# Rows of every expert slot turned by DMA under the shared expert, and loaded three slots ahead

## The chip, the core and the metric

The kernel runs on one core of a Trainium2 chip. The time is the device time of one execution in microseconds (us). Several runs of a kernel differ by a few us (three runs of this one: 2012.39 to 2018.24), so the median counts. A profile is one execution with the hardware profiler. TensorE (PE in the profile) multiplies matrices, and its weight loads are listed apart (PEld); VectorE is DVE, ScalarE ACT, GpSimd POOL, and SyncE (SP) issues most plain DMAs. Results of TensorE lie in PSUM banks and must be read out by VectorE or ScalarE.

## What is computed

Four sequences of 1024 tokens, 1024 wide, pass a cross-attention and a mixture of experts. Cut to what matters here:

```python
x = x + xattn(layernorm(x), ctx, Wq, bq, Wk, bk)      # softmax over 1024 context rows
xt = layernorm(x).reshape(4096, 1024)
scores = sigmoid(xt @ gate_w.T)                        # 8 experts
_, sel = top_k(scores + expert_bias, 2)
sel_flat = sel.reshape(-1)
order = argsort(sel_flat, stable=True)                 # 8192 rows, sorted by expert
tok_idx = order // 2
routed_in = xt[tok_idx] * top_scores.reshape(-1)[order][:, None]
routed_out = grouped_swiglu(routed_in, w1, w2, w3, rows_per_expert)   # bf16, hidden 704
shared = silu(xt @ sw1.T) * (xt @ sw3.T) @ sw2.T       # float32
x = x + shared.at[tok_idx].add(routed_out)
```

## The kernel before

There are three stages, and TensorE works through them almost without a gap.

**Attention** (to about 640 us). 32 groups of 128 tokens are handled in 16 steps p of two groups. Beside the products (`product`, L401, with the seven block products of `seven`, L199) each step normalizes, routes, and scatters the weighted tokens as bf16 rows into the DRAM table `xrows`, in a region for each expert (`scatter`, L525; each row carries its token's number behind the 1024 values). `convert(e)` (L244) lets GpSimd issue three DMAs that copy expert e's float32 weights to bf16 tables in DRAM; L650 calls it in steps 1, 5, 9 and 13, for experts 0 to 3.

**Shared expert** (640 to 1473 us). 8 blocks s of 512 tokens (NJ = 8, loop at L1100), in float32. `up(s)` (L937) makes the hidden activations: one product for the tails (`pt_c`, 7.06 us) and five rounds f of the seven products with halves (12.09 us a round, 1.73 us a product). `down_pair(s, 0)` and `down_pair(s, 1)` (L1033) make the outputs, two sets of seven products, some 18 us each. `between(k)` is called after product k and puts the work of VectorE and ScalarE there. `block(s + 1)` (L154) loads the next block's tokens (`xb`) on SyncE's queue once `up(s)` has read the old ones, GpSimd forms sums of them (`differences`, L174), and `residuals(s)` (L996) loads 2 MB of `x2c` at round 1. Experts 4 to 7 are converted at L1134 in blocks 0 to 3, between the two down pairs.

Under this stage the rows of the expert stage are prepared by the generator `turns` (L1001). The routed rows are taken in 23 **slots** (NS) of 512 rows, each with one expert, each of four **turns** of 128 rows. A turn: GpSimd gathers 128 rows from `xrows` into `xgt` (four buffers, asked for two turns ahead; L750 is the line of every gather), VectorE takes the token numbers out of it (`toks`, L1022), and SyncE issues a DMA transpose of the 128 x 1024 values into half of `xh` (L1027). After two turns `xh` is stored to DRAM (L1019): the store stands in SyncE's queue ahead of the next turn's transpose, and waits for both transposes of its pair. L974 takes one turn after products 1 and 4 of each round, from block 2 on: 10 turns in each of six blocks, 60, the rows of slots 0 to 14 (NTURN = 15).

**Experts** (1473 us to the end; loop at L1176). Each slot is an up part (88 matmuls at L131, from the turned rows `xTb` and the gathered weights `w`) and a down part (L1161, L1167, L1169). A slot's row count sets the width of its matmuls at run time, so slots take 13 to 29 us. Two sets of buffers (`bps`) alternate. After its up part a slot issues: for slots below 15, on SyncE, the load of slot s+2's turned rows as two DMAs (`fetch_turned`, L906, L909), into the buffer that was just read; and on GpSimd the gather of slot s+2's w13 (`fetch_up`). GpSimd then adds the 512 output rows into `out` by indirect DMAs (L1208) and gathers w2 and w2t of slot s+2 (`fetch_down`). Gathers whose expert the buffer already holds move nothing. Slots 15 to 22 are not turned by DMA: `fetch_rows` (L882) gathers their rows into SBUF, and during the up part of the slot before, `turned_rows` (L911) lets TensorE transpose eight 128 x 128 pieces per turn through PSUM (L920), which VectorE copies out (L921).

TensorE, GpSimd, and in these stages VectorE, ScalarE and SyncE keep the order in which the program is written: an instruction that waits holds up all that are behind it on its engine or queue.

Of the kernel before, what the change touches and what calls it, by code (L numbers as in the profile page):

```python
# [29 lines left out]
BF16 = mybir.dt.bfloat16  # L34
# [26 lines left out]
EPS = 1e-5  # L61
LEAST = 32
ROW = D + 32
NTURN = 15


_WIDTHS = dict(ident=P, tri=P, ones=P, before=E * E, upto=E * E, region=E, expert=E, full=NJ,
# [12 lines left out]
def xattn_moe_kernel(ctx: ExitStack, tc: tile.TileContext, x, ctxT, wqT, wkT, bqk, gwT, ebias,  # L80
# [14 lines left out]
    def const(k):  # L95
        return con[:, _AT[k][0] : _AT[k][1]]

    ident = const("ident")
    identb, trib, onesb = (cp.tile([P, P], BF16, name=f"{k}b") for k in ("ident", "tri", "ones"))
    before = const("before").rearrange("p (i j) -> p i j", j=E)  # L100


# [14 lines left out]
    ps_t = ctx.enter_context(tc.tile_pool(name="ps_t", bufs=2, space=PSUM))  # L117
# [111 lines left out]
    with ExitStack() as a:  # L229
# [316 lines left out]
        load(0)  # L546
        with tc.manual_schedule(engines=vector_scalar):
            ps_e = psum("ps_e", 3)
            for dst, k in ((identb, "ident"), (trib, "tri"), (onesb, "ones")):
                nc.vector.tensor_copy(dst, const(k))  # L550
            halves = queries(0)
            tokens(0)
# [32 lines left out]
            for p in range(NT // 2):  # L585
# [35 lines left out]
                def between(k):  # L621
# [15 lines left out]
                    elif k == 1:  # L637
                        if new:
                            looked(i)
                            softened(i)  # L640
                        if not ahead:
                            gss[g - 2] = gate_parts(g - 2, xtTs.pop(g - 2))
                        elif p:
                            xtTs[g - 1] = turn(g - 1)
                        if ahead:
                            scaled(b + 1, i, on_scalar=True)
                        if p > 1:
                            tois, ss = listing.pop(g - 4)
                            listing[g - 4] = tois, [weighted(g - 4, j, ss) for j in range(G)]
                        if p % (NT // E) == 1:  # L650
                            convert(p // (NT // E))
                    elif k == 2:
                        if not ahead:
                            xtTs[g - 1] = turn(g - 1)
                        looked(i + 1)
                        softened(i + 1)
                        if g + 2 < NT:
                            norms[g + 2] = statistics(xin[g + 2], f"1_{g + 2}")
                        if g + 2 == NT:
                            two_sums.close()  # L660
                            cps.append(pool(shared, "c3"))
                            block(0)
                    elif k == 3:
                        if p:
                            gss[g - 1] = gate_parts(g - 1, xtTs.pop(g - 1))
                            lg = ps_s.tile([P, G, E], F32, tag="lg", name=f"lg_{g}")
                            gate(lg, g - 2, gss.pop(g - 2))
                        if ahead:
                            turned(b + 1, i)
                            scaled(b + 1, i + 1, on_scalar=True)  # L670
                        if p:
                            gate(lg, g - 1, gss.pop(g - 1))
                            routing[g - 2] = route(g - 2, lg)
                        if p > 1:
                            scatter(g - 4, *listing.pop(g - 4))
                        if g + 2 < NT:
                            norms[g + 3] = statistics(xin[g + 3], f"1_{g + 3}")
                    elif k == 4:
                        if ahead:
                            turned(b + 1, i + 1)  # L680
                    elif k == 5:
                        if g + 2 < NT:
                            tokens(g + 2)
                        if p:
# [71 lines left out]
    def tables(tb):  # L756
# [123 lines left out]
    weights, fetched, slots = [], {}, {}  # L880
# [22 lines left out]
    def xT_of(s):  # L903
        return bps[s % 2].tile([P, KC, SLOT], BF16, tag="xT", name=f"xTb_{s}")

    def fetch_turned(s):  # L906
        slots[s] = xT_of(s), tokens_of[s]
        for h in range(2):
            nc.sync.dma_start(slots[s][0][:, :, h * 2 * P : (h + 1) * 2 * P], xturned[s][h])  # L909

    def turned_rows(s, q):  # L911
        if q == 0:
            slots[s] = xT_of(s), bps[s % 2].tile([P, NQ], I32, tag="toks", name=f"toks_{s}", bufs=2)
        xT, toks = slots[s]
        xg = fetched[s][q]
        nc.vector.tensor_tensor(toks[:, q : q + 1], xg[:, D : D + 2].bitcast(I32),
                                beyond[:, s, q : q + 1], ALU.bitwise_or)
        pt = ps_t.tile([P, KC, P], BF16, tag="pt", name=f"ptb_{s}_{q}")
        for c in range(KC):
            nc.tensor.transpose(pt[:, c, :], xg[:, c * P : (c + 1) * P], identb)  # L920
        nc.vector.tensor_copy(xT[:, :, q * P : (q + 1) * P], pt)  # L921

    def widths(s):

# [7 lines left out]
    with shared, tc.manual_schedule(engines=vector_scalar | {mybir.EngineType.SP}):  # L932
# [4 lines left out]
        def up(s):  # L937
# [3 lines left out]
            for f in range(NF):  # L941
# [11 lines left out]
                def between(k):  # L953
# [46 lines left out]

        def turns():  # L1001

            blocks = list(itertools.product(range(NTURN), range(NQ)))
            asked = []

            def ask(s, q):
# [8 lines left out]
            for j, (s, q) in enumerate(blocks):  # L1015
# [10 lines left out]
                    xh = tr.tile([P, KC, 2 * P], BF16, tag="xh", name=f"xh_{s}_{h}", bufs=2)  # L1026
                nc.sync.dma_start_transpose(xh[:, :, v * P : (v + 1) * P], xg[:, :D])  # L1027
                if v:
                    done = xturned[s][h], xh
                yield  # L1030
            nc.sync.dma_start(*done)

        def down_pair(s, u, more=None):  # L1033
# [23 lines left out]
            def between(k):  # L1057
# [21 lines left out]
                if more:  # L1079
                    more(k)  # L1080

# [18 lines left out]
        for s in range(NJ):  # L1100
# [10 lines left out]
            if s + 1 == NJ:  # L1111
# [61 lines left out]
    fetch_turned(1)  # L1173
    fetch_up(1)
    fetch_down(1)
    for s in range(NS):  # L1176
        parts = nextparts
        w13_s, w2_s, w2t_s = weights[s % 2]
        xT, toks = slots.pop(s)
# [3 lines left out]
        for f, _ in enumerate(upwards(w13_s, lambda c: xT[:, c, :], hT, ring, bx, slot_tails,  # L1183
                                      f"b{s}", parts[0])):
# [118 lines left out]
```

## Time and profile before

| what | value |
|---|---|
| median of three runs | 2016.29 us |
| the three runs | 2012.39, 2016.29, 2018.24 us |
| the profiled execution's own time | 2016.26 us |
| its span (first to last instruction) | 2014.5 us |
| granted TensorE clock, mean | 0.992 |
| DMA, mean over the span | 169 GB/s |
| GpSimd's DMA queue, share of the 16 engines | 32.8% |
| SyncE's DMA queue, share of the 16 engines | 27.0% |

How its lines are read: a group's line has the source line, engine and operation, the tiles (out<-in), shape and count, then the busy time and the mean of one in ns, then the idle time of the engine just before, with what ended it. A timeline row has start and length in us, engine, line, operation, tiles, the count of merged instructions, and in brackets the idle time before it with its releaser. On SPq rows the length is that of the issue on SyncE's queue, not of the transfer. The DMA share of a stretch is the mean busy share of 16 DMA engines by the packets' own times; packets that overlap on an engine can bring it above 1.

### The profile page before, as it was taken

What the parts mean: (1) busy time and instruction counts of PE and PEld (TensorE: products, weight loads), DVE (VectorE), ACT (ScalarE), POOL (GpSimd) and SP (SyncE); (2) the same over time, 40 slices, a digit from 0 to 9 for tenths busy, and PEclk for the clock granted to TensorE, in tenths of its full rate; (3) what the DMA queues carried; (4) which work ended last, traced back from release to release, by engine and by line L of the source; (5) the groups of instructions that cost most, each with busy time, mean ns of one, the idle gap of its engine ahead of it and who ended that gap; (6) DMA issues with size and microseconds to landing.
All of it is one profiled execution on the core that took longest, in us unless ns stands there. A gap on an engine that the chain in (4) does not pass through costs nothing.

```text
span 2014.5 us, 24206 instructions
## 1 busy us (share of the span) xinstructions
PE 1961.7 (97%) x8992; PEld 1175.0 (58%) x9107; DVE 828.2 (41%) x2014; ACT 514.6 (26%) x900; POOL 650.2 (32%) x598
## 2 busy tenths in 40 slices
PE   8999999999999999999999999999999897999997
PEld 5555655655454448485858576767655553456665
DVE  5456566556863426313131313231333332224353
ACT  3344444454432101010101010101022232223232
POOL 0423433433642140312121212121124533256563
PEclk9999999999999999999999999999999998999999
DMA  4263473373765143595959272727646877489994
GB/s 122 85 172 116 150 197 117 119 209 135 243 204 210 64 114 98 149 221 138 211 141 239 84 204 80 194 90 188 237 99 127 247 194 226 102 216 334 297 306 81
DMA packets 179972, 340.37 MB, mean 169 GB/s; under 512 B 80400, under 2 KB 119824, under 8 KB 176016
## 3 DMA queue, kind: packets, MB, share of 16 engines
q0 software_dynamic: 43024, 172.78, 32.8%
q1 hardware_dynamic: 136832, 166.04, 27.0%
q8 instruction: 73, 1.20, 0.2%
q14 instruction: 43, 0.35, 0.1%
HBM read 280.80 MB, written 166.20 MB: 222 GB/s over the span
## 4 chain that ended last, share of the span: by engine, by line
PE 93%; DMA 3%; DVE 1%; issue 1%; ACT 0%; another core or an unknown queue 0%; POOL 0%; POOLq 0%; SPq 0%; DVEq 0%; ACTq 0%
PE pa L131 22%; PE bank L131 15%; PE pc L131 12%; PE bank L1169 6%; PE qa L131 6%; PE pb L131 6%; PE pu L131 4%; DMA xTb<-xturned 3%; PE pq L310 3%; PE qc L131 3%; PE pe L322 3%; PE pt_c L131 2%; PE pt_a L258 1%; PE qb L131 1%; PE pt_t L258 1%; PE pt_x L258 1%
## 5 line engine op out<-in xcount | busy, mean ns | idle before, releaser
L131 PE MATMUL bank<-xTb,w 128*128 128x0 bf16 x2024 | 318.9, 318 | 18.0 <-DMA xTb<-xturned 15.5
L131 PEld LDWEIGHTS <-w 128*128 128x128 bf16 x2024 | 190.8, 99 | 128.6 <-issue 22.7
L750 POOL DMA_INDIRECT xgt<-xrows,li x60 | 57.3, 955 | 431.8 <-DMA xh<-xgt 173.3
L1208 POOL DMA_INDIRECT out_dram<-yt,toks x92 | 146.7, 1595 | 115.7 <-DVE yt L1204 81.9
L1169 PE MATMUL bank<-w,hTb 128*128 128x0 bf16 x920 | 165.6, 327 | 3.1 <-DVE hTb L148 3.1
L275 POOL TENSOR_TENSOR rs<-ve,con 128x1 f32<-128x1 f32 x64 | 47.7, 745 | 321.7 <-DVE ve L273 318.0
L148 DVE TENSOR_TENSOR hTb<-sg_b,bank 128x512 bf16<-128x512 f32 x115 | 78.7, 687 | 162.7 <-PE bank L131 149.0
L131 PE MATMUL pa<-xs,sw_sb 128*128 128x256 f32 x560 | 132.3, 379 | 0.0
L1169 PEld LDWEIGHTS <-hTb 128*128 128x128 bf16 x920 | 72.2, 98 | 92.4 <-issue 13.7
L131 PE MATMUL pa<-aT,xT 128*128 128x512 f32 x256 | 116.8, 599 | 1.6 <-DVE x L412 1.4
L147 ACT ACTIVATE sg_b<-bank 128x512 f32<-128x512 f32 x115 | 68.4, 597 | 184.7 <-PE bank L131 158.7
L131 PEld LDWEIGHTS pa<-xs,sw_sb 128*128 128x128 f32 x560 | 106.4, 190 | 14.4
L1204 DVE COPY yt<-bank 128x512 f32<-128x512 f32 x92 | 61.6, 689 | 120.8 <-PE bank L1169 112.4
L1206 ACT COPY yt<-bank 128x512 f32<-128x512 f32 x92 | 53.5, 585 | 147.9 <-PE bank L1169 136.0
L964 DVE TENSOR_TENSOR one<-one,pb 128x256 f32<-128x256 f32 x35 | 14.7, 420 | 172.4 <-PE pb L131 172.4
L528 POOL DMA_INDIRECT xrows<-rr,toi x64 | 64.6, 1009 | 61.9 <-issue 40.1
L412 DVE SCALAR_TENSOR_TENSOR x<-pa,rs,x 128x512 f32<-128x512 f32 x64 | 47.8, 748 | 86.6 <-PE pa L131 80.6
L168 ACT ACTIVATE st_c<-pt_c 64x256 f32<-64x256 f32 x7 | 2.6, 377 | 311.8 <-PE pt_c L131 311.8
L1055 DVE TENSOR_TENSOR x2c<-x2c,qa 128x512 f32<-128x512 f32 x64 | 43.8, 685 | 93.5 <-PE qa L131 93.5
L268 DVE BATCH_NORM_STATS2 st<-x 128x6 f32<-128x512 f32 x128 | 81.8, 681 | 0.6
L750 POOL DMA_INDIRECT w<-w13b,wi x23 | 23.2, 1009 | 180.5 <-PE bank L131 152.7
L131 PE MATMUL pu<-xb,sw_sb 128*128 128x512 f32 x176 | 76.3, 594 | 0.9 <-PE pt_t L258 0.9
(268 smaller groups left out, 3445.0 us busy)
## 6 DMA issues: line engine op xcount, KB each, us to landing
w13b<-in_w_dram POOLq DMA_DIRECT2D x8, 2816.0 KB
x<-in_x_dram SPq DMA_DIRECT2D x32, 512.0 KB
x2d<-x SPq DMA_DIRECT2D x32, 512.0 KB
xtd<-xtT SPq DMA_DIRECT2D x32, 512.0 KB
xb<-xtd SPq DMA_DIRECT2D x8, 2048.0 KB
x2c<-x2d SPq DMA_DIRECT2D x16, 1024.0 KB
out_dram<-x2c SPq DMA_DIRECT2D x16, 1024.0 KB
xturned<-xh SPq DMA_DIRECT2D x30, 512.0 KB
```

The lines of the kernel that those rows point to most:

```text
L131: nc.tensor.matmul(part(pp), w(c), part(xT(c)), start=start and c == 0, stop=c == blocks - 1, skip_group_check=not start)
L147: nc.scalar.activation(sg, pa, AF.Silu)
L148: nc.vector.tensor_tensor(hT[:, f, :], sg, pb, ALU.mult)
L258: nc.tensor.transpose(pt[:, j, :], src[:, c * P : (c + 1) * P], ident)
L268: nc.vector.bn_stats(st[:, h, :], src[:, h * 512 : (h + 1) * 512])
L310: nc.tensor.matmul(pq[:, i, j, :], w[c // CH][:, c % CH, :], ct[c // CH][:, c % CH, :], start=c == 0, stop=c == CC - 1)
L322: nc.tensor.matmul(pe[:, h, :], qs[b][:, m * P : (m + 1) * P], ks[b][:, h * 512 : (h + 1) * 512], start=True, stop=True)
L528: nc.gpsimd.indirect_dma_start(out=places[2 * (g + i) + k], out_offset=bass.IndirectOffsetOnAxis(ap=tois[k][:, i : i + 1], axis=0), in_=rr ...
L750: nc.gpsimd.indirect_dma_start(out=dst, out_offset=None, in_=src, in_offset=bass.IndirectOffsetOnAxis(ap=idx, axis=0), **bound)
L1169: nc.tensor.matmul(part(py), hT[:, f, toks], part(w[:, f, cols]), start=False, stop=f == NF - 1, skip_group_check=q < 2)
L1204: nc.vector.tensor_copy(yt[:, q, h * 512 : (h + 1) * 512], py)
L1208: adds.append([nc.gpsimd.indirect_dma_start(out=outs[q], out_offset=bass.IndirectOffsetOnAxis(ap=toks[:, q : q + 1], axis=0), in_=yt[:, q, ...
```

## The change

- All 23 slots are turned under the shared expert: 92 turns, in place of 60. From block 2 on there is a turn after products 0, 2 and 4 of each round (15 in an up part) and one after product 3 of each down pair (two a block): 17 a block in place of 10.
- `xturned` of a slot is one DRAM tile of 128 x 8 x 512, so a pair's store writes runs of 512 bytes, and a slot's load is one DMA whose runs are 8 KB for each partition. Before, stores had runs of 4 KB, and each of two loads had runs of 512 bytes in SBUF.
- The turned rows have a pool of their own with three buffers (`bt`): slots 0 to 2 are asked for before the last block's down part, and slot s+3 after the up part of slot s.
- `fetch_rows`, `turned_rows`, the transposes on TensorE, their PSUM copies and the bf16 identity are gone from the expert stage.
- Weight conversions: six in attention (steps 1, 3, 5, 7, 10, 13) and two in blocks 0 and 1, in place of four and four.

```diff
-NTURN = 15
...
-    tokens_of = [cp.tile([P, NQ], I32, name=f"toks_{i}") for i in range(NTURN)]
-    xturned = [[dram.tile([P, KC, 2 * P], BF16, name=f"xturned_{i}_{h}") for h in range(2)]
-               for i in range(NTURN)]
+    tokens_of = [cp.tile([P, NQ], I32, name=f"toks_{i}") for i in range(NS)]
+    xturned = [dram.tile([P, KC, SLOT], BF16, name=f"xturned_{i}") for i in range(NS)]
...
-                        if p % (NT // E) == 1:
-                            convert(p // (NT // E))
+                        if p in (1, 3, 5, 7, 10, 13):
+                            convert((1, 3, 5, 7, 10, 13).index(p))
...
-    def fetch_rows(s):
-        bp = bps[s % 2]
-        fetched[s] = [bp.tile([P, ROW], BF16, tag=f"xg{q}", name=f"xg_{s}_{q}") for q in range(NQ)]
-        for q, xg in enumerate(fetched[s]):
-            gather(xg.bitcast(I32), xrows, li[:, s, q : q + 1])
...
     def fetch_turned(s):
-        slots[s] = xT_of(s), tokens_of[s]
-        for h in range(2):
-            nc.sync.dma_start(slots[s][0][:, :, h * 2 * P : (h + 1) * 2 * P], xturned[s][h])
-
-    def turned_rows(s, q):
...
-        pt = ps_t.tile([P, KC, P], BF16, tag="pt", name=f"ptb_{s}_{q}")
-        for c in range(KC):
-            nc.tensor.transpose(pt[:, c, :], xg[:, c * P : (c + 1) * P], identb)
-        nc.vector.tensor_copy(xT[:, :, q * P : (q + 1) * P], pt)
+        slots[s] = bt.tile([P, KC, SLOT], BF16, tag="xT", name=f"xTb_{s}")
+        nc.sync.dma_start(slots[s], xturned[s])
...
-                    if s > 1 and k in (1, 4):
+                    if s > 1 and k in (0, 2, 4):
                         next(turning, None)
...
-            blocks = list(itertools.product(range(NTURN), range(NQ)))
+            blocks = list(itertools.product(range(NS), range(NQ)))
...
-                    done = xturned[s][h], xh
+                    done = xturned[s][:, :, h * 2 * P : (h + 1) * 2 * P], xh
...
+                if s > 1 and k == 3:
+                    next(turning, None)
                 if more:
                     more(k)
...
                 bps.append(pool(ctx, "b0", 1, "right"))
+                bt = pool(ctx, "bt", 3, "right")
                 fetch_turned(0)
                 fetch_up(0)
                 fetch_down(0)
+                fetch_turned(1)
+                fetch_turned(2)
...
-            if E // 2 + s < E:
-                convert(E // 2 + s)
+            if s < 2:
+                convert(E - 2 + s)
...
-                if f and s + 1 >= NTURN:
-                    turned_rows(s + 1, f - 1)
-        if NTURN <= s + 3 < NS:
-            fetch_rows(s + 3)
-        if s + 2 < NTURN:
-            fetch_turned(s + 2)
+        if s + 3 < NS:
+            fetch_turned(s + 3)
         if s + 2 < NS:
             fetch_up(s + 2)
```

More of the change, by code (lines that the diff above doesn't have):

```diff
@@ L98, in xattn_moe_kernel @@
     ident = const("ident")
-    identb, trib, onesb = (cp.tile([P, P], BF16, name=f"{k}b") for k in ("ident", "tri", "ones"))
+    trib, onesb = (cp.tile([P, P], BF16, name=f"{k}b") for k in ("tri", "ones"))
     before = const("before").rearrange("p (i j) -> p i j", j=E)
@@ L110, in xattn_moe_kernel @@
     beyond = cp.tile([P, NS, NQ], I32, name="beyond")
-    tokens_of = [cp.tile([P, NQ], I32, name=f"toks_{i}") for i in range(NTURN)]
-    xturned = [[dram.tile([P, KC, 2 * P], BF16, name=f"xturned_{i}_{h}") for h in range(2)]
-               for i in range(NTURN)]
+    tokens_of = [cp.tile([P, NQ], I32, name=f"toks_{i}") for i in range(NS)]
+    xturned = [dram.tile([P, KC, SLOT], BF16, name=f"xturned_{i}") for i in range(NS)]
     places = bass_types.dram_disjoint_views(xrows, 2 * NT)
-    ps_t = ctx.enter_context(tc.tile_pool(name="ps_t", bufs=2, space=PSUM))
+    transposes = ctx.enter_context(ExitStack())
+    ps_t = transposes.enter_context(tc.tile_pool(name="ps_t", bufs=2, space=PSUM))
     shared = ctx.enter_context(ExitStack())
@@ L548, in xattn_moe_kernel @@
             ps_e = psum("ps_e", 3)
-            for dst, k in ((identb, "ident"), (trib, "tri"), (onesb, "ones")):
+            for dst, k in ((trib, "tri"), (onesb, "ones")):
                 nc.vector.tensor_copy(dst, const(k))
@@ L879, in tables @@
         nc.vector.tensor_copy(beyond, over)
-    weights, fetched, slots = [], {}, {}
-    def fetch_rows(s):
-        bp = bps[s % 2]
-        fetched[s] = [bp.tile([P, ROW], BF16, tag=f"xg{q}", name=f"xg_{s}_{q}") for q in range(NQ)]
-        for q, xg in enumerate(fetched[s]):
-            gather(xg.bitcast(I32), xrows, li[:, s, q : q + 1])
+    weights, slots = [], {}
     def fetch_up(s):
@@ L901, in fetch_down @@
                oob_is_err=False)
-    def xT_of(s):
-        return bps[s % 2].tile([P, KC, SLOT], BF16, tag="xT", name=f"xTb_{s}")
     def fetch_turned(s):
-        slots[s] = xT_of(s), tokens_of[s]
-        for h in range(2):
-            nc.sync.dma_start(slots[s][0][:, :, h * 2 * P : (h + 1) * 2 * P], xturned[s][h])
-    def turned_rows(s, q):
[L912 to L917, printed above, removed]
-        pt = ps_t.tile([P, KC, P], BF16, tag="pt", name=f"ptb_{s}_{q}")
-        for c in range(KC):
-            nc.tensor.transpose(pt[:, c, :], xg[:, c * P : (c + 1) * P], identb)
-        nc.vector.tensor_copy(xT[:, :, q * P : (q + 1) * P], pt)
+        slots[s] = bt.tile([P, KC, SLOT], BF16, tag="xT", name=f"xTb_{s}")
+        nc.sync.dma_start(slots[s], xturned[s])
     def widths(s):
@@ L1172, in xattn_moe_kernel @@
     outs, adds = bass_types.dram_disjoint_views(out, NQ), []
-    fetch_turned(1)
     fetch_up(1)
@@ L1178, in xattn_moe_kernel @@
         w13_s, w2_s, w2t_s = weights[s % 2]
-        xT, toks = slots.pop(s)
+        xT, toks = slots.pop(s), tokens_of[s]
         hT = bx.tile([P, FC, SLOT], BF16, tag="hT", name=f"hTb_{s}")
@@ L1182, in xattn_moe_kernel @@
         coming, nextparts = widths(min(s + 1, NS - 1)), []
-        for f, _ in enumerate(upwards(w13_s, lambda c: xT[:, c, :], hT, ring, bx, slot_tails,
-                                      f"b{s}", parts[0])):
+        for _ in upwards(w13_s, lambda c: xT[:, c, :], hT, ring, bx, slot_tails, f"b{s}", parts[0]):
             if s + 1 < NS:
                 nextparts.append(next(coming))
-                if f and s + 1 >= NTURN:
-                    turned_rows(s + 1, f - 1)
-        if NTURN <= s + 3 < NS:
-            fetch_rows(s + 3)
-        if s + 2 < NTURN:
-            fetch_turned(s + 2)
+        if s + 3 < NS:
+            fetch_turned(s + 3)
         if s + 2 < NS:
```

## The prediction

> **What bounds the kernel now.** The page comes first. Its part 1 says that TensorE is busy in 1961.7 of 2014.5 us, so only what shortens TensorE's work or its waits moves the end; part 5 names the largest wait.
>
> ```profile
> PE 1961.7 (97%) x8992; PEld 1175.0 (58%) x9107; DVE 828.2 (41%) x2014; ACT 514.6 (26%) x900; POOL 650.2 (32%) x598
> ...
> L131 PE MATMUL bank<-xTb,w 128*128 128x0 bf16 x2024 | 318.9, 318 | 18.0 <-DMA xTb<-xturned 15.5
> ```
>
> The second line: the expert products sat idle 18.0 us, 15.5 of it until a slot's turned rows (xTb) had landed. The timeline of TensorE puts this in two places, before slots 6 and 9 (slots counted from 0; a slot begins with x88 matmuls of L131 and goes down from its first L1161).
>
> ```profile
> 1608.13 16.98 PE L131 MATMUL bank<-xTb,w 128*128 128x0 bf16 x88 [5.54 <-DMA xTb<-xturned]
> 1625.04 0.61 PE L1161 MATMUL bank<-w2t,hTb 64*128 64x512 bf16 x4
> ...
> 1632.80 14.46 PE L131 MATMUL bank<-xTb,w 128*128 128x0 bf16 x88
> ...
> 1647.19 0.60 PE L1161 MATMUL bank<-w2t,hTb 64*128 64x512 bf16 x4
> ...
> 1678.40 20.69 PE L131 MATMUL bank<-xTb,w 128*128 128x0 bf16 x88 [10.01 <-DMA xTb<-xturned]
> 1699.02 0.61 PE L1161 MATMUL bank<-w2t,hTb 64*128 64x512 bf16 x4
> ```
>
> The brackets give waits of 5.54 and 10.01 us. Slot 6 then needs 16.91 us to its L1161, its equal, slot 7, 14.39: the granted clock was 0.89 over 1608 to 1633. The same timeline further on shows the equal of slot 9 (slot 11), and a slot in which TensorE turns rows (slot 14; L920, eight transposes a row):
>
> ```profile
> 1738.20 19.16 PE L131 MATMUL bank<-xTb,w 128*128 128x0 bf16 x88
> 1757.29 0.60 PE L1161 MATMUL bank<-w2t,hTb 64*128 64x512 bf16 x4
> ...
> 1822.27 0.61 PE L920 MATMUL ptb<-identb,xg 128*128 128x128 bf16 x8
> 1822.71 2.76 PE L131 MATMUL bank<-xTb,w 128*128 128x0 bf16 x16
> ...
> 1831.41 0.61 PE L920 MATMUL ptb<-identb,xg 128*128 128x128 bf16 x8
> 1831.95 0.61 PE L1161 MATMUL bank<-w2t,hTb 64*128 64x512 bf16 x4
> ```
>
> **Transposes taken off TensorE.** The order of the changed program has the same TensorE instructions, without these 256. A group holds the next row back by 0.44 (1822.27 to 1822.71), 0.45, 0.45 and 0.54 us: 1.88 us a slot, in slots 14 to 21: 8 x 1.88 = **15.0 us**. (The group's busy sum, 20.0 us, counts overlapping ends.) Slot 19 is short and also shows seven waits of 0.2 to 1.2 us around its groups, 4.1 us in all; their releasers are the copies of VectorE and ScalarE, from which 32 turned-row copies of 0.68 us go. Between 0 and 4.1 I take 1.
>
> The Trainium skill speaks against this edit: VectorE: DVE Perf Modes, "The three transpose paths", gives a 128x128 bf16 transpose as 390 ns on TensorE and 1309 ns by DMA, and advises TensorE where PSUM will do. By it, 256 transposes would free 100 us of TensorE and 32 more blocks of eight would take 335 us of DMA. Here TensorE's groups cost 15.0 us in all, and a pair of DMA turns (16 such transposes) lands in 5.6 to 10.5 us; the rows decide.
>
> **The waits for xTb.** On SyncE's queue the loads for slots 6 and 7 begin where slot 4 has read its buffer, and the four issues alone take 28 us:
>
> ```profile
> 1576.74 28.20 SPq L909 DMA_DIRECT2D xTb<-xturned  x4
> ```
>
> The chain has this load at 30.7 us, and that for slot 9 at 30.4, while a slot's expert weights cross (128 rows of 22.5, 10.2 and 2.0 KB, 4.5 MB); in quiet slots one issue takes 0.5 to 0.6. With three buffers slot s+3's load starts when slot s has been read. The shortest lead is then slot 20's: from slot 17's L1161 (1900.99) to 1940.82 is 40 us, some 34 when the transposes are gone; that is over 30.7 even if the load were as slow as before, and it is now one DMA with runs of 8 KB in place of 2 x 1024 packets of 512 B. So 5.54 + 10.01 = **15.6 us** go, and with them the slow restarts: 16.91 - 14.39 = 2.52 and 20.62 - 19.09 = 1.53, **4.0 us**. What is late next are the weights: they are asked for at the same places as before (w13 at 1576.98 for slot 6, 1647.54 for slot 9), and the last of their 22.5 KB packets in the trace ended at 1588.0 and 1659.0, before those slots could begin (1602.6, 1668.4). No new wait there.
>
> **The turning under the shared expert.** This is where the change can lose. It goes from 10 turns a block of 103.5 us to 17: 15 in the up part, which has 5 x 12.09 us, so one pair per 8.06 us, and two in the down pairs. Each turn issues a gather (POOL, 0.95 us), a tokens operation (VectorE, 0.15 us), a DMA transpose and half a store (SyncE, 1.2 to 8.3 and 0.33 us). POOL and VectorE have room; but SyncE's stores wait for both transposes of a pair before the next pair is issued, so a pair's length is the rate:
>
> ```profile
> 994.33 0.34 SPq L1019 DMA_DIRECT2D xturned<-xh  x1
> 994.78 6.07 SPq L1027 DMA_TRANSPOSE xh<-xgt  x2
> 1004.81 0.32 SPq L1019 DMA_DIRECT2D xturned<-xh  x1
> ...
> 1190.71 0.33 SPq L1019 DMA_DIRECT2D xturned<-xh  x1
> 1191.13 4.41 SPq L1027 DMA_TRANSPOSE xh<-xgt  x2
> 1198.39 0.32 SPq L1019 DMA_DIRECT2D xturned<-xh  x1
> ```
>
> Store to store, 10.5 us where both gathers start with the pair and 7.7 where they are spread. Beside the 2 MB of residuals a pair takes 13.3, beside a weight conversion 12 to 14. A turn that is late makes VectorE wait at its tokens operation, in order before the operations that empty TensorE's banks. A gather needs the transpose four turns earlier and then about 4 us. So turn 14 of a block, due at 7.06 + 4 x 12.09 + 5 x 1.73 = 64.1 us from the block's start, needs turn 11, the end of the sixth pair: 1.8 (start) + 7.2 + 13.3 + 4 P, then 4. With P = 9.7 (the mean of five pairs of 9.1 to 10.5 that had both gathers beside them) that is 65.1. VectorE may be 5 us late there: the results that it owes next are wanted at the down part's second product, at 70.9, after four operations of 0.42. So nothing is lost up to P = 10.7, and beyond it 4 us a block for each us of P, in five blocks. Bounds: 0 (P of 7.7), and 46 us (P of 13). I take **3 us**, most of it in block 2, whose first pair meets the end of block 1's conversion (12.9 in place of 7.2).
>
> Queued behind the turns on SyncE is the next block's xb load; it was issued at 1020.2 and its sums on POOL ended at 1038.9, while the first product that reads them comes 28 us later. The DMA share shows that there is room on average:
>
> ```profile
> 850.00:954.00 104.00, 104.00 (x388) 70.76 (x386) 28.85 (x69) 10.87 (x28) 20.69 (x17) 1.00 0.76 181
> ...
> 1161.00:1264.50 103.50, 103.50 (x386) 70.73 (x384) 28.79 (x69) 10.87 (x28) 18.82 (x14) 1.00 0.50 138
> ...
> 1840.00:1865.00 25.00, 25.00 (x206) 16.62 (x212) 12.45 (x24) 9.73 (x18) 17.95 (x17) 1.00 1.03 339
> ```
>
> (Stretch, length, busy time of PE, PEld, DVE, ACT, POOL, granted clock, DMA share, GB/s.) A block with ten turns and no conversion has 0.50, one with a conversion 0.76 with TensorE at 103.5 of 103.5. Seven more turns at some 3.5 us of all engines make 0.50 + 24.5 / 103.5 = 0.74.
>
> **The conversions.** Two go from under blocks 2 and 3 to attention, four places become six. Each is 1.9 us of POOL and 24 to 30 us of DMA; the stretches they go into (150 to 200, 300 to 350, 450 to 500) have a DMA share of 0.29 to 0.32 and TensorE busy 50.00 of 50, and in the 50 us after each of the four old ones TensorE's longest wait was 0.41 us. Cost 0; without that cover 1.9 us each. The dropped identity copy and the gathers saved in slots 12 to 19 are off the path.
>
> **The late slots.** Slots 14 to 19 run at a DMA share of 0.83 to 1.03. From 1796 to 1940 the stretches moved 44.5 MB, 309 GB/s; with 12 us less it would be 337, and the best stretch shows 339. The load that comes closest is slot 20's w13 (landed 1935.6, read at 1940.8); with the slots before it shorter I count a slack of 3 us. I take **1 us**; the bound is the whole 12.
>
> **Sum**, from the profiled execution's own 2016.26 us (span 2014.5; the median of the three runs is 2016.29, so both agree): 2016.26 - 15.0 - 1 - 15.6 - 4.0 + 3 + 1 = 1984.7, so **1985 us**.
>
> **Rivals.**
> 1. The late slots become DMA-bound: 9 to 12 of the 16 us there stay, 1994 to 1998. For: the share of 1.03. Against: TensorE never waits for weights there now. Chance 0.13.
> 2. Turning falls somewhat behind: P of 11.2 to 11.8 costs 4 x 0.5 x 5 = 10 to 22 us in place of 3, 1992 to 2004. For: five pairs of 9.1 to 10.5 close to the limit. Against: without conversions the pairs were 5.6 to 7.7. Chance 0.12.
> 3. **Slower**: the same place, if pairs stay at 13 and more as beside a conversion, all blocks through: 4 x 2.3 x 5 = 46, 2028. The gain of 34.6 is used up at P = 12.4. Chance 0.06.
> 4. The loads do not come in time although asked for earlier, since weights are served first: of the four gains only 16 us come, less 3 and 1: 2004. Against: a lead of 34 us and more against 30.7. Chance 0.07.
>
> My forecast has 0.62 (1976 to 1992). Below 1974 nothing leads; up to 2006 all but rival 3 and the tail of 2 are inside. A difference under 0.3% (6 us) can't be told from none here: faster 0.91, same 0.03, slower 0.06.
>
> **What would show it.** L920 gone and slot 14 at 22 us in place of 23.9; no wait on xTb, and slots 6 and 9 at the length of 7 and 11; in blocks 2 to 6 a DMA share of 0.7 to 0.8, TensorE without waits, and VectorE's idle time before the tokens operations under 5 us each. Waits of TensorE in the up part or behind it with idle VectorE at the tokens mean rivals 2 and 3; waits for w at slots 15 to 21 mean rival 1.

## The result and the profile after

The changed kernel takes **1979.12 us** (median of four runs, 1977.36 to 1979.86) against 2015.9 for the kernel before beside it: a ratio of 0.9818, with a 95% interval of 0.9801 to 0.9835. Its profiled execution took 1977.36 us, with a span of 1975.6 and a mean granted clock of 0.997: 38.9 us of span less than the 2014.5 shown before.

The page, part 1 and the group of the expert products:

```profile
PE 1940.2 (98%) x8736; PEld 1157.9 (59%) x8851; DVE 809.3 (41%) x1981; ACT 514.4 (26%) x900; POOL 651.7 (33%) x598
...
L129 PE MATMUL bank<-xTb,w 128*128 128x0 bf16 x2024 | 310.6, 315 | 3.1 <-issue 1.3
```

256 TensorE instructions are gone, and the expert products (now L129) sat idle 3.1 us in place of 18.0, none of it for xTb. The timeline of TensorE for slots 6, 9 and 14, whose rows the prediction showed:

```profile
1604.19 14.46 PE L129 MATMUL bank<-xTb,w 128*128 128x0 bf16 x88
1618.59 0.61 PE L1142 MATMUL bank<-w2t,hTb 64*128 64x512 bf16 x4
...
1661.51 19.15 PE L129 MATMUL bank<-xTb,w 128*128 128x0 bf16 x88
...
1792.62 14.46 PE L129 MATMUL bank<-xTb,w 128*128 128x0 bf16 x88
1807.02 0.61 PE L1142 MATMUL bank<-w2t,hTb 64*128 64x512 bf16 x4
```

No bracket stands ahead of slots 6 and 9, and their up parts take 14.46 and 19.15 us, as their equals always did. Slot 14 runs its 88 products in one row, with no transposes between. What the turning costs is seen in the stretches of blocks 2, 3 and 6 (stretch, length, busy time of PE, PEld, DVE, ACT, POOL, granted clock, DMA share, GB/s):

```profile
850.00:954.00 104.00, 102.01 (x379) 70.00 (x378) 28.90 (x76) 10.76 (x28) 25.78 (x21) 1.00 0.82 209
952.00:1056.00 104.00, 104.00 (x387) 71.12 (x386) 29.72 (x77) 10.88 (x28) 25.57 (x21) 1.00 0.72 188
...
1264.00:1368.00 104.00, 104.00 (x387) 71.06 (x386) 29.77 (x76) 10.87 (x28) 25.44 (x21) 1.00 0.77 193
```

Blocks 3 to 6 are as long as before (103.49 us from start to start), with a DMA share of 0.72 to 0.78, and the last block has 105.60 us to the first slot in place of 105.39; only block 2, at 0.82, took 106.29.

Start to start, in the two profiled executions, the 38.9 us come from these places:

| place | before | after | difference, us |
|---|---|---|---|
| slots 14 to 21, sum of the eight differences | | | -15.9 |
| slots 5 and 8, with the waits ahead of slots 6 and 9 | 23.73, 23.44 | 18.04, 13.01 | -16.1 |
| slots 6 and 9 themselves | 24.67, 30.67 | 22.15, 29.13 | -4.1 |
| slot 13 | 19.30 | 14.58 | -4.7 |
| block 2 | 103.49 | 106.29 | +2.8 |
| the rest (attention, last block, last slot) | | | -0.9 |

### The profile page after: what moved, and what is told of

The parts are those of the page before. It is cut to its first block, busy times and chain, and to the rows that moved or that the text cites. A ratio compares the mean times of both kernels' runs of the same rounds, so it can differ in the third digit from the quotient of the medians.

```text
span 1975.6 us, 23759 instructions
## 1 busy us (share of the span) xinstructions
PE 1940.2 (98%) x8736; PEld 1157.9 (59%) x8851; DVE 809.3 (41%) x1981; ACT 514.4 (26%) x900; POOL 651.7 (33%) x598
## 4 chain that ended last, share of the span: by engine, by line
PE 91%; DMA 3%; DVE 2%; issue 1%; SPq 1%; POOL 1%; ACT 0%; POOLq 0%; DVEq 0%; ACTq 0%
PE pa L129 21%; PE bank L129 15%; PE pc L129 11%; PE bank L1150 7%; PE qa L129 6%; PE pb L129 5%; PE pu L129 4%; PE pq L308 3%; PE qc L129 3%; PE pe L320 3%; PE pt_c L129 2%; DMA xh<-xgt 2%; PE pt_a L256 1%; PE qb L129 1%; PE pt_t L256 1%; PE pt_x L256 1%
## 5 line engine op out<-in xcount | busy, mean ns | idle before, releaser
L129 PE MATMUL bank<-xTb,w 128*128 128x0 bf16 x2024 | 310.6, 315 | 3.1 <-issue 1.3
L129 PEld LDWEIGHTS <-w 128*128 128x128 bf16 x2024 | 189.2, 98 | 111.7 <-issue 1.0
L748 POOL DMA_INDIRECT xgt<-xrows,li x92 | 88.2, 959 | 439.8 <-DMA xh<-xgt 169.1
L129 PE MATMUL pa<-xs,sw_sb 128*128 128x256 f32 x560 | 132.4, 380 | 0.3 <-DVE five L943 0.3
L129 PE MATMUL pa<-aT,xT 128*128 128x512 f32 x256 | 116.8, 599 | 1.5 <-DVE x L410 1.4
L129 PEld LDWEIGHTS pa<-xs,sw_sb 128*128 128x128 f32 x560 | 106.5, 190 | 14.9 <-DVE five L943 0.7
L129 PE MATMUL pu<-xb,sw_sb 128*128 128x512 f32 x176 | 76.3, 594 | 0.9 <-PE pt_t L256 0.9
L129 PEld LDWEIGHTS pa<-aT,xT 128*128 128x128 f32 x256 | 46.3, 191 | 48.8 <-issue 47.8
```

Of the source, the lines that this page charges most:

```text
L129: nc.tensor.matmul(part(pp), w(c), part(xT(c)), start=start and c == 0, stop=c == blocks - 1, skip_group_check=not start)
L748: nc.gpsimd.indirect_dma_start(out=dst, out_offset=None, in_=src, in_offset=bass.IndirectOffsetOnAxis(ap=idx, axis=0), **bound)
```

## The experiments

Theory: three sums that hardly touch each other. The loads of the turned rows come in time (some 20 us), TensorE is rid of its transposes (some 15), and the turning of 92 turns fits under six blocks. Rivals: that the load's gain hangs on one of its two edits alone (three buffers with a longer lead, or whole runs of 8 KB); that the conversions, costed at nothing, decide whether the turning fits; and that the turning is bound by the DMA engines' share and not by the length of a pair. All kernels compute the whole result. The kernel before, run beside each set, had medians of 2013.99, 2016.31 and 2014.73 us.

**Two slots ahead, whole runs kept** (e1).

```diff
-                bt = pool(ctx, "bt", 3, "right")
+                bt = pool(ctx, "bt", 2, "right")
...
-                fetch_turned(2)
...
-        if s + 3 < NS:
-            fetch_turned(s + 3)
+        if s + 2 < NS:
+            fetch_turned(s + 2)
```

> The changed kernel, but with two buffers of turned rows in place of three, each slot's load asked for two slots ahead as before the change; the whole runs in DRAM stay. Theory A (the runs of 8 KB cured the waits): the changed kernel's loads landed 4.7 to 12.0 us after their issue, and two slots ahead still leaves at least 18 us, so no wait on xTb comes back: 1979 us. Theory B (the longer lead cured them): a load beside the weights takes 30 us again and waits of some 5 and 10 us come back before slots 6 and 9, with slow restarts of 4 us: 1995 to 1999 us, more if late slots wait too.

Measured: 1979.51 us (1973.78 to 1984.1), ratio 0.9824 [0.9798, 0.9851]; no wait on xTb. The third buffer is worth nothing that can be measured here: with whole runs, two are enough.

**Three ahead, but in halves** (e2): the old layout, two DMAs a slot with runs of 512 bytes.

```diff
-    xturned = [dram.tile([P, KC, SLOT], BF16, name=f"xturned_{i}") for i in range(NS)]
+    xturned = [[dram.tile([P, KC, 2 * P], BF16, name=f"xturned_{i}_{h}") for h in range(2)]
+               for i in range(NS)]
...
-        nc.sync.dma_start(slots[s], xturned[s])
+        for h in range(2):
+            nc.sync.dma_start(slots[s][:, :, h * 2 * P : (h + 1) * 2 * P], xturned[s][h])
...
-                    done = xturned[s][:, :, h * 2 * P : (h + 1) * 2 * P], xh
+                    done = xturned[s][h], xh
```

> The changed kernel, but with the old form of the turned rows in DRAM (two halves per slot, so a slot is loaded by two DMAs whose runs are 512 bytes in SBUF); the lead of three slots stays. Theory A (both cures work alone): loads take up to 31 us beside the weights, against leads of 34 us and more: 1979 us, at most 5 us more where a late slot's load is slower still. Theory B (512-byte runs are served last as long as weights cross): waits on xTb in the late slots, where weights cross all the time: 1985 to 2000 us.

Measured: 2014.6 us (2009.74 to 2030.57, ten runs), ratio 1.0009 [0.9988, 1.0031]. **The whole gain is gone**, though all transposes are off TensorE and every load has a lead of three slots. The waits before slots 6 and 9 have vanished, and two longer ones stand before slots 16 and 20. (Block 2 took 109.96 us in this profile, 3.7 more than in the changed kernel and 4.2 more than in e3, which stores the same halves; why stays open.) First TensorE's timeline, then what the trace answers on the tile xTb (issue to landing of the 46 halves):

```profile
1847.51 2.72 PE L130 MATMUL bank<-xTb,w 128*128 128x0 bf16 x6 [13.86 <-DMA xTb<-xturned]
...
1942.41 3.04 PE L130 MATMUL bank<-xTb,w 128*128 128x0 bf16 x9 [19.05 <-DMA xTb<-xturned]
```

```profile
DMA to landing us min/median/max: 3.8/7.7/55.6
```

A half of 512 KB lands in some 4 us at best, and mostly in 25 to 56 us when weights and output rows cross. Why, the DMA view of the stretch from 1807 to 1847 shows (queue, packets, MB, share of the time of 16 engines):

```profile
q0 software_dynamic: 2072, 12.00, 92.1%
q1 hardware_dynamic: 2389, 1.21, 11.8%
```

GpSimd's queue (q0) and SyncE's (q1) got through about the same number of packets, 2072 and 2389, but q0's carried 12.00 MB and q1's 1.21. The kernel before shows the same from 1582 to 1606 us, under the load that holds up slot 6, with equal counts:

```profile
q0 software_dynamic: 1005, 7.40, 93.3%
q1 hardware_dynamic: 1005, 0.51, 8.5%
```

By an estimate from the rows of e2, a packet of 512 bytes waited on the average for one of 5.8 KB, which holds an engine 0.921 x 40 x 16 / 2072 = 0.28 us; 1024 packets over 16 engines are 64 x 0.28 = 18 us for a half that is alone in its queue, and the halves queue behind each other. In the changed kernel a slot's 1 MB is 128 packets, 8 turns an engine. This agrees with the Trainium skill, DMA: Bandwidth & Descriptors, "Queues, rings and completion order": each DMA engine goes round the queues that have work, a packet at a time. (The page's packets hold some 9 to 17 descriptors; those that the profile counts here are single runs.)

**Halves, and two ahead** (e3): the edits of e1 and e2 together, so the old way of loading, now for all 23 slots.

> The changed kernel with both the old form (two halves, 512-byte runs) and the old lead (two slots, two buffers): only the turning of all slots by DMA and the moved conversions are left of the change. If the gain is the sum as predicted, the waits and slow restarts come back: 1979 + 5.5 + 10 + 4 = 1999 us. Rival: slots 15 to 22 now depend on such loads too, where weights cross for every slot, and more waits come: 2005 to 2040 us.

Measured: 2047.74 us (2041.17 to 2058.14), ratio 1.0156 [1.0124, 1.0187], slower than before and beyond the rival's 2040 us too. Waits on xTb of 5.4 to 22.3 us before slots 6, 9, 14, 16, 18 and 20: the slots from 15 on, which had their rows from GpSimd's gathers before, now wait too. With e1, e2 and the changed kernel this makes four corners: whole runs 1979 (three ahead) and 1980 (two); halves 2015 and 2048. The lead is worth 33 us with halves and nothing with whole runs; the run length is worth 35 to 68.

**Two DMAs of 4-KB runs** (e9), to part the size of the packets from the number of DMAs in e2.

```diff
-        nc.sync.dma_start(slots[s], xturned[s])
+        for h in range(2):
+            nc.sync.dma_start(slots[s][:, h * KC // 2 : (h + 1) * KC // 2],
+                              xturned[s][:, h * KC // 2 : (h + 1) * KC // 2])
```

> The changed kernel, with a slot's turned rows loaded by two DMAs of 128 x 4 KB runs in place of one of 128 x 8 KB. The run with halves had two DMAs of 1024 runs of 512 bytes and lost the whole gain. Theory A, the number of packets is what made those loads late: 256 packets of 4 KB land about as fast as 128 of 8 KB (4.7 to 12 us), no wait on xTb, 1979 with 4 us either way. Theory B, two DMAs in a row on SyncE's queue are what made them late: waits on xTb in slots 15 to 20 come back in part, 1990 to 2014.

Measured: 1977.71 us (1976.36 to 1978.77), ratio 0.9815 [0.9799, 0.9832], no wait on xTb, landings of 3.8 to 16.5 us. Theory A: not the second DMA, the packets.

**The new loads alone** (e4): the kernel before (slots 0 to 14 turned by DMA, the others on TensorE, conversions four and four), with only the DRAM layout, the single load and the three buffers of the change (and, for space, one pool in place of two for the row buffers of slots 15 to 22).

```diff
-    xturned = [[dram.tile([P, KC, 2 * P], BF16, name=f"xturned_{i}_{h}") for h in range(2)]
-               for i in range(NTURN)]
+    xturned = [dram.tile([P, KC, SLOT], BF16, name=f"xturned_{i}") for i in range(NTURN)]
...
-        for h in range(2):
-            nc.sync.dma_start(slots[s][0][:, :, h * 2 * P : (h + 1) * 2 * P], xturned[s][h])
+        nc.sync.dma_start(slots[s][0], xturned[s])
...
-        if s + 2 < NTURN:
-            fetch_turned(s + 2)
+        if s + 3 < NTURN:
+            fetch_turned(s + 3)
```

> The kernel before with only the loads changed: three buffers, three slots ahead, whole runs, for slots 0 to 14; slots 15 to 22 are still turned by TensorE and the conversions stay (the row buffers of slots 15 to 22 lie in one pool in place of two, for space). If the gain is the sum as predicted, 15.6 of waits and 4.0 of slow restarts go: 2016 - 19.6 = 1996 us. If slot 13's wait of 4.7 us on ScalarE, which the changed kernel does not show, hangs on these loads as well: 1992 us. Rival, that the waits move to the weights: above 2005 us.

Measured: 1989.27 us (1985.07 to 1989.81), ratio 0.9877 [0.9861, 0.9894]. Of the 37 us, the loads alone bring some 25; moving the last 32 turns and the conversions adds the other 10 to 12, not 15: slots 14 to 18, 20 and 21 keep their transposes, 1.8 us each, but slot 19 took 11.2 us here against 12.26 in the changed kernel (0.72 of it the wait for slot 20's weights), and the changed kernel's block 2 costs 2.8 (in the two profiled executions the difference of the spans is 7.7). Slot 13 is at 14.58 us here, as in the changed kernel.

**The kernel before, profiled a second time** (b2), for two differences that no step had foreseen: slot 13's, and the small waits of slot 19.

> The kernel before, profiled a second time. In its first profile slot 13 took 19.3 us, with 3.8 us in which ScalarE waited on something that the profile doesn't name; in the changed kernel it took 14.6. Theory A: that wait belongs to the kernel (its traffic just there), and slot 13 takes 19 us again. Theory B: it falls on one execution or another, and slot 13 takes about 14.6 us here. Slots 6 and 9 wait for xTb again, 5.5 and 10 us, in both.

Measured: 2011.56 us (one run). Slots 6 and 9 wait again (4.94 and 11.15 us), so those waits belong to the kernel. Slot 19, 15.01 us in the first profile, took 11.36: its seven waits come in one execution and not in another. Slot 13 is long again (18.99 us against 19.30), but by another wait. In the first profile of before the engines stand so in slot 13, ScalarE's row ahead of TensorE's:

```profile
1808.64 0.60 ACT L147 ACTIVATE sg_b<-bank 128x512 f32<-128x512 f32 x1 [3.77 <-remote]
```

```profile
1810.02 1.25 PE L1169 MATMUL bank<-w,hTb 128*128 128x0 bf16 x5 [2.07 <-DVE hTb L148]
```

ScalarE stood for 3.77 us with a releaser that the profile can't name, VectorE's hTb was late, and TensorE with it, which then had a granted clock of 0.50 from 1812 to 1814 us. In b2 ScalarE has no such wait in slot 13. TensorE stands at its end, ahead of slot 14; with that row, what the trace answers on slot 14's two loads:

```profile
1813.90 6.35 PE L131 MATMUL bank<-xTb,w 128*128 128x0 bf16 x28 [4.25 <-DMA xg<-xrows,li]
```

```profile
L909 SPq DMA_DIRECT2D xTb<-xturned x2: 518/594/669, 1785.0 to 1785.5; - x2
DMA to landing us min/median/max: 4.0/16.1/28.2
```

The row names xg, which these products don't read. They read xTb, and its second half, issued at 1785.53, landed 28.2 us later, 0.14 us before TensorE went on, the same 0.14 as after the landings for slots 6 and 9. So in b2 slot 13's time is a third late load, before slot 14, and e3, with the old loads, waits for xTb at the same place. It goes with the new loads (e4, and every kernel here that has them). In the first profile slot 14 began 28.7 us after its second load was issued, so a load as slow would have been hidden behind ScalarE's wait; what released ScalarE there stays open.

**All conversions back at their old places** (e5), four in attention and four under blocks 0 to 3.

```diff
-                        if p in (1, 3, 5, 7, 10, 13):
-                            convert((1, 3, 5, 7, 10, 13).index(p))
+                        if p in (1, 5, 9, 13):
+                            convert((1, 5, 9, 13).index(p))
...
-            if s < 2:
-                convert(E - 2 + s)
+            if s < 4:
+                convert(E - 4 + s)
```

> The changed kernel with the conversions where they were: four in attention, four under blocks 0 to 3. Blocks 3 and 4 now also begin beside a conversion as block 2 does. Theory A (a late turn holds up VectorE, and through it TensorE): blocks 2, 3 and 4 each lose some 3 us as block 2 alone did (106.3 in place of 103.5): 1979 + 6 = 1985 us. By the working of the prediction with pairs of 13 us throughout it would be 9 us a block: 1997. Theory B (the place of the conversions does not matter): 1979 us.

Measured: 1991.26 us (1989.66 to 1994.38), ratio 0.9882 [0.9867, 0.9897]: 12 us slower than the changed kernel, between the two expectations. Blocks 2, 3 and 4 take 107.35, 107.64 and 109.27 us, the later ones 103.49. The stretches of blocks 3, 4 and 5, columns as above:

```profile
957.40:1065.00 107.60, 105.40 (x386) 71.76 (x385) 29.27 (x77) 10.87 (x28) 27.58 (x24) 0.98 0.91 226
1065.00:1174.30 109.30, 104.59 (x386) 70.41 (x385) 29.36 (x77) 10.76 (x28) 25.55 (x21) 1.00 0.83 210
1174.30:1277.80 103.50, 103.50 (x386) 70.72 (x385) 29.38 (x77) 10.88 (x28) 25.69 (x21) 1.00 0.74 189
```

A conversion that ran beside ten turns without loss costs 4 to 6 us beside seventeen. Blocks 2, 3 and 4 each begin beside the end of one, which lands 12, 16 and 14 us into the block; why block 4 loses most stays open.

**All eight conversions in attention** (e6).

```diff
-                        if p in (1, 3, 5, 7, 10, 13):
-                            convert((1, 3, 5, 7, 10, 13).index(p))
+                        if p in (1, 3, 4, 6, 7, 9, 10, 13):
+                            convert((1, 3, 4, 6, 7, 9, 10, 13).index(p))
...
-            if s < 2:
-                convert(E - 2 + s)
```

> The changed kernel with all eight conversions in attention (steps 1, 3, 4, 6, 7, 9, 10, 13) and none under the shared expert. Theory A: block 2 then takes 103.5 us like the others, and attention has room for two more: 1979 - 3 = 1976 us. Theory B (block 2 is long for another reason, such as its residuals' load or the start of turning): 106 us again, 1979 us. Attention would show it if two more cost anything there: its end at 640 us moves.

Measured: 1978.09 us (1975.7 to 1981.76), ratio 0.9813 [0.98, 0.9827]. Block 2 is back at 103.49, so its 2.8 us were the end of block 1's conversion. But the shared expert begins 2.2 us later in this profile (631.9 against 629.7) and slot 20 waits 1.75 us for its weights in place of 0.72: the total can't be told from the changed kernel's. That attention ends later isn't shown to be the two conversions' doing: its longer waits of TensorE are those of the changed kernel, and after one of them (525.9) the same eight products took 5.28 us in place of 3.67, at a granted clock of 0.50. With six conversions, e1, e3, e7 and e8 too reach block 1 some 2.2 to 2.5 us later than the changed kernel.

**The tokens operation one turn later** (e7): VectorE takes a turn's token numbers out at the next turn, so that a late gather no longer holds what is behind it.

```diff
                 xg = asked.pop(0)
-                nc.vector.tensor_tensor(tokens_of[s][:, q : q + 1], ...
+                if late:
+                    tokens_out(*late)
+                late = s, q, xg
```

> The changed kernel, with VectorE's tokens operation of a turn taken one turn later (its buffer is held that much longer); the transposes and gathers stay as they are. Theory A: VectorE's waits of up to 6.5 us before the tokens operations in block 2 are what TensorE's 2.8 us there come from; a turn later the gather has landed, and block 2 takes about 103.5 us: 1976 us. Theory B: TensorE waits there for the engines' DMA load by some other way (sums, residuals), and block 2 stays at 106 us: 1979 us.

Measured: 1980.25 us (1979.01 to 1983.03), ratio 0.9824 [0.9811, 0.9837]. Block 2 took 103.49 again, so the path is shown: turning late, gather late, VectorE waits at the tokens operation, TensorE waits for VectorE. In the changed kernel's block 2 that is, on VectorE and then on TensorE:

```profile
895.64 0.16 DVE L998 TENSOR_TENSOR toks<-xgt,beyond 128x1 int32<-128x1 int32 x1 [5.16 <-DMA xgt<-xrows,li]
...
903.53 0.16 DVE L998 TENSOR_TENSOR toks<-xgt,beyond 128x1 int32<-128x1 int32 x1 [5.94 <-DMA xgt<-xrows,li]
```

```profile
920.74 1.99 PE L129 MATMUL qc<-vs,hs 128*128 128x512 f32 x4 [0.52 <-DVE hs L176]
```

The gain does not show in the total: block 1 begins 2.4 us later in this profile, the last block has 107.05 us to the experts in place of 105.60, and slot 20 waits 2.14 us for its weights.

**Every DMA transpose issued twice** (e8), to find where the turning ceases to fit.

```diff
                 nc.sync.dma_start_transpose(xh[:, :, v * P : (v + 1) * P], xg[:, :D])
+                nc.sync.dma_start_transpose(xh[:, :, v * P : (v + 1) * P], xg[:, :D])
```

> The changed kernel, with every DMA transpose of the turning issued twice (the second writes the same values to the same place). Theory A, the prediction's formula: the length of a pair sets the rate, nothing is lost up to 10.7 us a pair, and 4 us a block for each us beyond, in five blocks. Pairs that follow each other without a pause take 7.5 to 7.9 us in the changed kernel; two more transposes add something between 3 (the shortest issue-to-store stretch for two) and 5.5 us, so pairs of 10.7 to 13.4 and a loss of 0 to 54 us: 1979 to 2033, and the loss of each block must agree with 4 x (P - 10.7) for the P read in it. Theory B: what counts is the DMA share of the block, 0.72 to 0.82 now and still below 1 with the doubled transposes, so blocks 3 to 7 stay at 103.5 whatever the pairs' length: 1979 to 1985.

Measured: 2182.96 us (2182.53 to 2185.79), ratio 1.0841 [1.0823, 1.0859]: 204 us slower than the changed kernel, far beyond both theories. The line of the page that carries it, and block 3 by its stretch:

```profile
L129 PE MATMUL pa<-xs,sw_sb 128*128 128x256 f32 x560 | 161.6, 440 | 133.1 <-DVE five L943 133.1
```

```profile
993.50:1134.00 140.50, 111.08 (x386) 74.50 (x384) 29.09 (x76) 10.64 (x28) 26.33 (x22) 0.91 0.73 173
```

The DMA share is 0.73, as in the changed kernel's blocks without loss, and the block is 37 us longer: **theory B falls**. What has grown is the pair. SyncE's queue in the changed kernel and in e8, store to store:

```profile
890.64 0.52 SPq L995 DMA_DIRECT2D xturned<-xh  x1
891.25 4.39 SPq L1003 DMA_TRANSPOSE xh<-xgt  x2
898.19 0.51 SPq L995 DMA_DIRECT2D xturned<-xh  x1
```

```profile
927.15 0.51 SPq L995 DMA_DIRECT2D xturned<-xh  x1
927.77 1.95 SPq L1003 DMA_TRANSPOSE xh<-xgt  x1
933.16 1.23 SPq L1004 DMA_TRANSPOSE xh<-xgt  x1
934.44 1.34 SPq L1003 DMA_TRANSPOSE xh<-xgt  x1
937.62 1.23 SPq L1004 DMA_TRANSPOSE xh<-xgt  x1
941.72 0.51 SPq L995 DMA_DIRECT2D xturned<-xh  x1
```

7.55 us became 14.57: each second issue (L1004) writes what the first wrote, and here it starts 5.4 and 3.2 us after it. Beside a load of residuals a pair took up to 23.3 (stores at 1446.05 and 1469.36). A chain of waits of this kind leaves the DMA share as it was, so the share tells nothing of it. Theory A is right on the cause and wrong on the price: at P = 14.8, the usual pair with nothing beside it, its formula gives 4 x 4.1 = 16 us a block, and blocks 2 to 6 lost 35 to 44. No pair in them is shorter than 14.56 us, so none catches up, and a block lasts as long as its 8.5 pairs: the five blocks took 714.3 us for 42.5 pairs, 16.8 us each. From this one can estimate that blocks grow at the latest when the mean pair passes 103.5 / 8.5 = 12.2 us. No run tests a mean near that, and a shorter one is no safeguard: the changed kernel's block 2 lost 2.8 us although its first seven pairs, to the store at 921.65, took 10.3 us each.

## Why the prediction was right, point by point

- **Transposes off TensorE, 15.0 + 1:** measured 15.9, slot by slot. Seven slots gave 1.77 to 2.24 us, so 1.88 a slot was the right reading of the gaps. Slot 19 gave 2.75, but only because its waits fell on the first profile (15.01 us) and not on the second (11.36, against 12.26 after). So the term is 13.1 us in seven slots and -0.9 to 2.8 in the eighth, by the execution; the 1 for slot 19's waits can't be confirmed, and that the whole came to 15.9 is in part luck.
- **Waits for xTb, 15.6, and slow restarts, 4.0:** measured 16.1 and 4.1. The sum was right, but **a step of its reasoning failed**: "that is over 30.7 even if the load were as slow as before". e2 has that lead and the old packets. There the step holds for slots 6 and 9 and fails for the late slots, where output rows and weights leave no quiet stretch and the loads queue behind one another: those of slot 20, the shortest lead by the prediction, landed 33.0 and 51.5 us after their issue, and the slowest of all after 55.6. Rival 4, at 2004, was put down with the same argument, and without the run length, which the prediction named second, the time would have been beyond it (2014.6). e1 and e9 show the reverse: run length is enough, lead is not needed.
- **Turning, 3:** measured 2.8, in block 2, and at the end of block 1's conversion, as forecast (e6). Yet its inputs were off. The pair that follows without a pause takes 7.5 to 7.9 us in block 2, not 9.7, and block 2's second pair, beside the residuals, 18.4 and not 13.3 (stores at 864.64 and 882.99). The errors, some 5 us too little and 8 too much, pull against each other at turn 14, which is luck: the sixth pair ends at 913.81, 64.3 us into the block, the gather lands at 918.6, 5.0 us after the turn is due, just at the 5 that were granted, and four waits of TensorE of 0.3 to 0.6 us, two of them before that turn, show 2.0 us of the loss. One of the signs named was off with it: VectorE's waits before the tokens operations were to stay under 5 us, and three in block 2 had 5.2 to 6.5. And the price beyond the threshold, "4 us a block for each us of P", gives less than half of what e8 lost: it counts the four pairs up to turn 14, while a turning that can't catch up carries its lag through all pairs of a block. Rival 3, at 2028, stood on that price; e8 shows the mechanism to be real, and the changed kernel's pairs of 7.5 to 7.9 us, where nothing else crosses, are far from it.
- **Conversions, 0:** attention did not grow (the shared expert begins at 629.7 us in place of 630.9). But "cost 0" was half of the step: left where they were they would have cost 12 us (e5). The two conversions moved are what makes the turning fit under blocks 3 and 4, and no term of the sum said so.
- **Late slots, 1:** slot 20 waited 0.72 us for w13, as named. Rival 1 did not come; but the same place has 1.54 to 2.50 us in the profiles of e1, e5, e6 and e7, so it is near.
- **Missing from the sum:** slot 13, 4.7 us, in before's trace all along as a wait of 2.07 us (L1169) and the slow clock after it, which no step took up. By b2 the load for slot 14 is as late as those for slots 6 and 9, so the sum counted two late loads where that execution has three. With 0.9 from the rest, and the 1 us for late slots that is already in the slots' differences, it is most of the 7.3 us by which 1984.7 stands above the profiled execution.

## What to carry to other kernels

A load that shared the DMA engines with another queue's large packets was timed by its number of packets, not by its bytes (e2, e9): lay the data out in DRAM for the load in long runs, let the store that has time pay with short ones, and only then ask for it earlier. For work that is passed along a chain of waits (gather, transpose, store), compare the length of its links with the time there is for them, over the whole and over the busiest stretch; the DMA share looked the same at no loss and at 37 us a block (e8). When an edit is costed at nothing, ask what leaving it out would cost in the changed kernel.

## What the runs showed of the hardware that was not expected

- Two queues with work were served about packet for packet: 2389 packets of 512 bytes beside 2072 of 5.8 KB on the average, so one queue had a tenth of the other's bytes (e2); 1005 beside 1005 from 1582 to 1606 us in the kernel before.
- Storing with runs of 512 bytes in place of 4 KB cost little: a store of 512 KB landed after a median of 4.1 us in the changed kernel and 2.9 in e2.
- Short waits were enough to slow TensorE, at times. After a wait of 2.20 us in e5 it began again at 976.4, and the stretch from 978 to 980 us shows a granted clock of 0.50, that from 980 to 982 0.85, then 1.00; its first two products took 3.10 and 2.52 us in place of 1.89. After 2.07 us in slot 13 of the kernel before the clock was 0.50 too, while after 1.4 us in e5 (1107.4) it stayed at 1.00. The length of the wait does not decide alone, as one group of products in attention shows, in e6 (granted clock 0.50 from 526 to 528 us) and in the changed kernel (1.00):

```profile
525.93 5.28 PE L129 MATMUL pa<-aT,xT 128*128 128x512 f32 x8 [1.40 <-DVE x L410]
```

```profile
524.74 3.67 PE L129 MATMUL pa<-aT,xT 128*128 128x512 f32 x8 [1.38 <-DVE x L410]
```

The Trainium skill, TensorE: Matmul & The Clock Gate, "What's actually happening", puts the fall to half the clock after an idle window of about 3.4 us; in these rows shorter waits did it. In block 3 of e8 waits of 8.0 and 9.5 us were followed by some 3 us at 0.50 to 0.53, and by the busy time of PE (111.08 us there in place of 104.00, up to 114.68 in block 2) its blocks lost 7 to 11 us to the clock on top of the waits.
